# Held loads, spaced GpSimd work, later step sizes, and two expert tiles returned by TensorE

## The chip, the cores and the metric

The kernel runs on one core of one Trainium2 chip. Its engines are TensorE (PE in the profile, PEld for its weight loads), VectorE (DVE), ScalarE (ACT), GpSimd (POOL) and SyncE (SP, which here only issues DMAs). The metric is device time in microseconds of one execution. Times are compared as medians of several runs.

## The reference

The input x has 1024 tokens of 512 features, all in fp32. Six residual blocks follow, each on a layer-normalized x; the expert layer appears twice with the same weights.

```python
x = x + 0.5 * _L0_ffn_ref(_layernorm(x), W_gate, b_gate, W_e, b_e)      # f0
x = x + _L0_attn_ref(_layernorm(x), wq, wkv, wo)                        # 32 heads, causal
x = x + 0.5 * _L0_ffn_ref(_layernorm(x), W_gate, b_gate, W_e, b_e)      # f1
x = x + 0.5 * _L1_ffn_ref(_layernorm(x), W_up, gate_w, ..., lora_B)     # up projection + LoRA expert
x = x + _L1_attn_ref(_layernorm(x), in_proj_w, ..., out_proj_w)         # Mamba, 64 heads, 8 groups
x = x + 0.5 * _L1_ffn_ref(_layernorm(x), W_up, gate_w, ..., lora_B)

def _L0_ffn_ref(x, W_gate, b_gate, W_e, b_e):          # 8 experts, two per token
    logits = x @ W_gate + b_gate
    _, top_idx = jax.lax.top_k(logits, 2)
    y_all = jax.nn.relu(jnp.einsum('bsd,edh->bseh', x, W_e) + b_e)
    y = jnp.take_along_axis(y_all, top_idx[..., None], axis=2)
    return y.mean(axis=2)
```

In the Mamba block the step size of each token and head is `dt_p = softplus(dt + dt_bias)` and its decay `exp(dt_p * A)`, with `dt` a projection to 64 columns; a scan over the tokens uses both.

## The kernel before

x stays in chip memory as eight tiles of 128 tokens (`x`), and `hT` holds the transposed, normalized x (four blocks of 128 features by 1024 tokens). `wpool` has four buffers of 1 MB for weights, `psml` four PSUM banks and `pbig` two double ones. Instructions are written in one text, but their order on an engine is worked out when the program is built: an instruction may go ahead of one that stands earlier in the text, unless `queue_behind` (one behind another) or `keep_in_program_order` pins it.

**An expert layer** (`expert_ffn`, tag f0 or f1) computes only the chosen experts. The normalized rows are stored to the DRAM tensor `rows`. DVE computes for every token its two experts and a place in a list of rows sorted by expert and padded to tiles of 128, the slot tiles. There are at least 16 slot tiles (`NS0`) and at most 23 (`NS`); a chain of `tc.If` skips those that are not used. `token` (L537) says for each slot which row to take, and `gather` (L543) fetches a tile's rows by an indirect DMA on POOL's queue; an unused place gets row 0. `turn` (L558) transposes a tile on PE and `slot_tile` (L593) multiplies it by its expert's weights, chosen by a register: eight PE instructions of 512 columns, a bias addition on DVE (L610), ReLU on ACT (L616) and a store to the DRAM tensor `outs` (L617). Tiles run in the order of their numbers. A tile's expert lies within bounds, so tile s up to 7 needs experts 0 to s loaded, and later ones all eight.

In f0, `gates_of_input` issues all loads on SP's queue: experts 0 to 3, then the row stores with experts 4, 5 after the fourth and 6, 7 after the eighth, then the biases, 2 MB spread over the partitions. The attention's first weights (`load_first`) are held back by `hold` (L160): a small memset into the tile on POOL, pinned to its place in POOL's queue, which the load must wait for. `meanwhile` is a list of pieces of other work: `load_first`, then two scalings of w_q (L806) and four sums or differences (L781) on POOL. The loop over the tiles takes one after tile 1 and one after each even tile from 4. After tile 2, SP also writes finite values into the rows of `outs` that belong to tiles 16 to 22, from x (L627).

**The way back.** `collect` (L667) makes a pipeline over the eight token tiles, used by the attention's first value projection after f0 and by the LoRA layer after f1: per tile two indirect gathers from `outs` (`gather_row`, L652), two additions into x on DVE (`add_pair`, L683), normalization (`normalize`, with the root as a power on POOL, L173), a transpose into `hT`, and then the next layer's products.

**The Mamba block** (`mamba`) goes over 16 units, a group of eight heads by half the sequence, four chunks of 128 tokens each. A unit begins with five `project_pair` calls (16 PE instructions of 512 columns each), of which three end in a convolution and SiLU (`conv_silu`: ACT, then DVE L1310), and `finish_bc`. Each chunk has `prepare` (the decays read back from DRAM into `dd`, a scan on DVE for `e_seg`, L1414) and `scan` (products, y). Ahead of the units, the pipeline after f1 ends in `add_bias` (L1253), which collects the step sizes; after token tile 3 and after tile 7 it calls `steps_of_time(q)` (L1185) for its half of the sequence: softplus and decays on DVE and ACT, three cumulative sums (`ps_cum`) and eight transposes on PE, and two stores to DRAM (`decay`) on SP's queue. Only after that does the text load group 0 and begin unit 0 (`load_group(0)` and five `project_pair`, at the end of `mamba`). The pools `w2` (xdt, xw, y and others) and `ep` (dd, e, cs) are opened after the pools of the step sizes are closed, on the memory these leave.

Of the kernel before, what the change touches and what calls it, by code (L numbers as in the profile page):

```python
# [22 lines left out]
P = 128  # L23
S = 1024
D = 512
# [11 lines left out]
NS0 = 2 * S // P  # L37
NE1 = 4
# [38 lines left out]
def macaron_kernel(  # L77
# [32 lines left out]
    rows = dram.tile([S, D], F32, tag="rows", name="rows")  # L110
# [49 lines left out]
    def hold(w):  # L160

        tc.keep_in_program_order(nc.gpsimd.memset(w[0:1, :, 0:1], 0.0))

    def weights(src, name, held=False):
        w = wpool.tile([P, KT, D], F32, tag="w", name=name)
        if held:
            hold(w)
        nc.sync.dma_start(w, src.rearrange("(k p) c -> p k c", p=P))
        return w
# [156 lines left out]
    def store_rows(t, xn):  # L326
        nc.scalar.dma_start(rows[t * P : (t + 1) * P, :], xn)

    def gate_steps(keep=store_rows, own=None):
# [6 lines left out]
        )  # L336

    def expert_ffn(tag, meanwhile, behind_weights=lambda: None):
# [5 lines left out]
        with tc.tile_pool(name=f"{tag}wa", bufs=1) as wap, tc.tile_pool(  # L344
# [16 lines left out]
            def gates_of_input():  # L361


                def keep(t, xn):
                    tc.keep_in_program_order(
                        nc.sync.dma_start(rows[t * P : (t + 1) * P, :], xn)
                    )
                    if t % 4 == 3:
                        for e in range(4 + t // 2 - 1, 4 + t // 2 + 1):
# [14 lines left out]
            behind_weights()  # L384

# [17 lines left out]
            nc.gpsimd.iota(lane_i, pattern=[[0, 1]], base=0, channel_multiplier=1)  # L403
# [137 lines left out]
            gathered, turned = {}, {}  # L541

            def gather(s):  # L543
                if s < NS0 + 3:
# [3 lines left out]
                nc.gpsimd.indirect_dma_start(  # L548
# [4 lines left out]
                    bounds_check=S - 1,  # L553
# [4 lines left out]
            def turn(s):  # L558
                xs = gathered.pop(s)
                ps = transposes(lambda i: xs[:, i * P : (i + 1) * P], KT)  # L560
                if s < NS0:
# [6 lines left out]
            for s in range(2):  # L568
                gather(s)

# [21 lines left out]

            def slot_tile(s):  # L593
                if s + 1 < NS:
                    turn(s + 1)
# [5 lines left out]
                for k in range(KT):  # L601
# [6 lines left out]
                    )  # L608
                y = wk.tile([P, D], F32, tag="y", name="y_e")
                nc.vector.tensor_tensor(  # L610
                    y,
                    ps,
                    b_all[:, bass.ds(ev, 1), :].rearrange("p e c -> p (e c)"),
                    ALU.add,
                )
# [1009 lines left out]
```

## Time and profile before

| | |
|---|---|
| median of 3 runs | 2866.86 us (2865.0 to 2867.82) |
| the profiled execution | 2867.5 us; its span 2865.8 us |
| PE busy | 2757.0 us (96%), mean granted clock 0.983 |
| DVE, ACT, POOL busy | 1747.1, 700.7, 901.6 us |
| DMA, mean over the span | 69 GB/s |
| slot tiles that ran (stores `outs<-y_e`) | 40: 19 in f0 and 21 in f1 |

A line of the timeline or of the groups reads: start in us and duration, engine, line of the kernel, operation, written tile <- read tiles, sizes, how many instructions; in brackets the idle time of that engine just before it and what ended it. PEq, SPq and the like are an engine's sequencer. A fp32 product of 128x128 by 128x512 is two instructions. POOL's DMA_INDIRECT is the issue of a gather, not its landing. The granted clock is 1.0 when PE runs at full speed.

### The profile page before, as it was taken

The page shows a single profiled execution, that of the slowest core. Times are in us where ns is not written, and L with a number is a line of the kernel's source. Part 1 is how long each engine was busy: PE and PEld are TensorE (multiplying, and loading weights), DVE is VectorE, ACT ScalarE, POOL GpSimd, SP SyncE. Part 2 cuts the span into 40 slices and gives each one's busy share as a digit, 9 for nine tenths or more (in the row PEclk, how much of TensorE's full clock was granted, in tenths as well). Part 3 has the DMA queues.
Part 4 walks back from the last instruction along what each step waited for, and adds up shares of the span by engine and source line. Part 5 has one row for each costly group of instructions (what it writes and reads, how often), then busy time and mean ns, then how long its engine had stood idle before and what let it go on. Part 6 is the DMA issues. An engine that isn't in the chain of part 4 may idle for free. (4 is left out here: it accounts for less than half of the span.)

```text
span 2865.8 us, 30223 instructions
## 1 busy us (share of the span) xinstructions
PE 2757.0 (96%) x11027; PEld 1567.6 (55%) x11027; DVE 1747.1 (61%) x3203; ACT 700.7 (24%) x1368; POOL 901.6 (31%) x749
## 2 busy tenths in 40 slices
PE   5799999999999999999999779999999999999998
PEld 3345566665666656666555434455555555555554
DVE  3256555665555656556555236767777776767673
ACT  2222221222222222212222224322223232222320
POOL 4322112221121212212200330355554545555451
PEclk8899999999999999999999889999999999999999
DMA  9411001010100101001014431223232222223210
GB/s 349 128 41 30 15 22 38 16 30 15 32 28 15 30 15 44 15 15 30 15 37 176 129 114 55 91 76 117 91 100 81 102 97 89 96 88 117 96 45 30
DMA packets 99604, 197.28 MB, mean 69 GB/s; under 512 B 8112, under 2 KB 33888, under 8 KB 99200
## 3 DMA queue, kind: packets, MB, share of 16 engines
q1 hardware_dynamic: 84944, 161.08, 17.1%
q0 software_dynamic: 6304, 20.47, 2.7%
q10 hardware_dynamic: 8208, 13.78, 1.3%
q8 instruction: 90, 1.47, 0.2%
q14 instruction: 58, 0.48, 0.1%
HBM read 176.17 MB, written 19.14 MB: 68 GB/s over the span
## 5 line engine op out<-in xcount | busy, mean ns | idle before, releaser
L855 PE MATMUL ps_s<-kT,qT 128*128 128x512 f32 (+3 forms) x768 | 292.8, 488 | 0.1
L879 PE MATMUL ps_o<-pT,v 128*128 128x512 f32 (+3 forms) x768 | 258.6, 486 | 0.2 <-ACT pT L900 0.2
L900 ACT COPY pT<-ps_tr 128x256 f32<-128x256 f32 (+2 forms) x192 | 91.7, 478 | 646.9 <-PE ps_tr L181 635.1
L869 ACT ACTIVATE pr<-ps_s,nm 128x128 f32<-128x128 f32 (+7 forms) x256 | 190.4, 744 | 238.4 <-DVE nm L866 208.0
L1509 PE MATMUL ps_out<-w_out,yg 128*128 128x512 f32 x512 | 237.2, 606 | 1.0 <-DVE yg L1472 1.0
L1439 POOL TENSOR_TENSOR cs<-cT,dd 128x1024 f32<-128x1024 f32 x56 | 181.9, 3248 | 167.9 <-PE ps_y L1457 139.6
L267 PE MATMUL ps_in<-hT,w_g 128*128 128x512 f32 x512 | 225.8, 594 | 1.5 <-ACT dt_ln L1196 1.5
L267 PE MATMUL ps_in<-hT,w_x 128*128 128x512 f32 x512 | 225.4, 592 | 0.0
L879 PEld LDWEIGHTS ps_o<-pT,v 128*128 128x128 f32 x768 | 143.5, 190 | 144.8 <-issue 98.8
L866 DVE TENSOR_REDUCE nm<-ps_s 128x1 f32<-128x128 f32 (+7 forms) x256 | 192.5, 753 | 3.9
L181 PEld LDWEIGHTS ps_tr<-ident,pr 128*128 128x128 f32 x1152 | 136.2, 141 | 76.3 <-issue 44.9
L181 PE MATMUL ps_tr<-ident,pr 128*128 128x128 f32 x1152 | 170.6, 275 | 4.3 <-DVE pr L871 3.2
L871 DVE TENSOR_SCALAR pr<-pr,sm 128x128 f32<-128x128 f32 (+7 forms) x256 | 165.6, 647 | 7.4
L267 PEld LDWEIGHTS ps_in<-hT,w_x 128*128 128x128 f32 x512 | 97.1, 190 | 121.2 <-issue 121.0
L267 PEld LDWEIGHTS ps_in<-hT,w_g 128*128 128x128 f32 x512 | 96.5, 190 | 121.6 <-issue 119.3
L1414 DVE TENSOR_TENSOR_SCAN e_seg<-dd,eye 128x1024 f32<-128x1024 f32 x64 | 154.5, 2414 | 6.4 <-PE ps_y L1457 6.3
L1310 DVE SCALAR_TENSOR_TENSOR xc<-ps_in,conv,xc 128x511 f32<-128x511 f32 (+2 forms) x192 | 141.7, 738 | 18.3 <-ACT xc L1306 17.9
L855 PEld LDWEIGHTS ps_s<-kT,qT 128*128 128x128 f32 x768 | 127.5, 192 | 39.9 <-issue 26.8
L1509 PEld LDWEIGHTS ps_out<-w_out,yg 128*128 128x128 f32 x512 | 93.0, 192 | 94.8 <-issue 94.3
L953 POOL TENSOR_TENSOR so<-oT 128x256 f32<-128x256 f32 x28 | 20.0, 725 | 380.2 <-DVE oT L886 336.7
L1433 POOL TENSOR_TENSOR xw<-xdt,erev 128x512 f32<-128x512 f32 x56 | 59.3, 1059 | 244.9 <-DVE xdt L1427 215.1
L806 POOL TENSOR_SCALAR w_q<-w_q 128x1024 f32<-128x1024 f32 x16 | 44.3, 2771 | 291.5 <-DMA w_q<-in_wq_dram 291.1
(290 smaller groups left out, 4823.7 us busy)
## 6 DMA issues: line engine op xcount, KB each, us to landing
dd<-decay SPq DMA_DIRECT2D x128, 512.0 KB, 4.6
w_all<-in_w_e_dram SPq DMA_DIRECT2D x16, 1024.0 KB, 12.4
outs<-y_e ACTq DMA_DIRECT2D x40, 256.0 KB, 3.6
w_v<-in_wkv_dram SPq DMA_DIRECT2D x8, 1024.0 KB, 5.2
w_q<-in_wq_dram SPq DMA_DIRECT2D x32, 256.0 KB, 4.2
w_k<-in_wkv_dram SPq DMA_DIRECT2D x8, 1024.0 KB, 5.2
w_o<-in_wo_dram SPq DMA_DIRECT2D x8, 1024.0 KB, 5.2
w_x<-in_in_wt_dram SPq DMA_DIRECT2D x8, 1024.0 KB, 7.8
```

Source lines behind the costliest of these rows:

```text
L181: nc.tensor.transpose(ps[:, i * P : (i + 1) * P], src(i), ident)
L267: nc.tensor.matmul(ps[:, cols : cols + n], lhsT=w[:, k, c0 : c0 + P], rhs=hT[:, k, t0 : t0 + n], start=(k == 0), stop=(k == KT - 1),)
L855: nc.tensor.matmul(ps[:, j : j + m], lhsT=qT[:, qt * P : (qt + 1) * P], rhs=kT[:, j : j + m], start=True, stop=True,)
L866: nc.vector.tensor_reduce(nm, ps[:, :n], AX.X, ALU.max, negate=True)
L869: nc.scalar.activation(pr[:, :n], ps[:, :n], AF.Exp, bias=nm, accum_out=sm)
L871: nc.vector.tensor_scalar(pr[:, :n], pr[:, :n], sm, None, ALU.mult)
L879: nc.tensor.matmul(ps[:, lo:512], lhsT=v[:, kb, hh * P : (hh + 1) * P], rhs=pT[:, kb, lo:512], start=(kb == 0), stop=(kb == last),)
L900: nc.scalar.copy(dst, src)
L1310: nc.vector.scalar_tensor_tensor(dst[:, s:], ps[:, : half - s], conv[:, ct, 3 - s : 4 - s], dst[:, s:], ALU.mult, ALU.add,)
L1414: nc.vector.tensor_tensor_scan(e.rearrange("p h l -> p (h l)"), dd[:, 0, :], eye8.rearrange("p h l -> p (h l)"), 0.0, ALU.mult, ALU.add,)
L1439: nc.gpsimd.tensor_tensor(cs, un["cT"][:, tok].unsqueeze(1).to_broadcast([P, HPG, P]), dd[:, 1, :].rearrange("p (h l) -> p h l", l=P), ALU ...
L1509: nc.tensor.matmul(po, lhsT=yg[:, k, :], rhs=w_o[:, k, :], start=(k == 0), stop=(k == 3))
```

## The change

- **Loads.** In f0 experts 6 and 7 and the biases leave the place among the row stores. They are issued after the first two gathers in the text, each behind a memset on POOL (`hold`, which now gets the slice to write).
- **GpSimd work.** In f0 the pieces of `meanwhile` behind `load_first` are taken one per tile from the eighth tile on, each pinned behind the gather that this step of the loop issues.
- **Two last tiles.** Slot tiles 6 and 7 (`LAST`), which are always in use, run after all others. Their gathered rows have buffers of their own, zeroed on POOL in f0; in f0 SP stores these zeros to their rows of `outs`, so that the two gathers of the way back fetch zeros for them. Their output is not stored: it stays in `hT` (`returned`). DVE builds matrices with a one where slot row and token belong together (`whose`, also in `hT`), and `return_last` adds the product of both to each token tile. `rows` gets a row 0 of its own and tokens count from 1, so that an unused place belongs to no token.
- **Step sizes.** `steps_of_time(1)` is called after the five `project_pair` and `finish_bc` of unit 0, which move ahead with `load_group`, `conv_silu` and the other helpers (their text is unchanged but for `in_line["conv"]`). The first scan of group 0 is pinned behind the last convolution.

```diff
+LAST = (6, 7)
-    rows = dram.tile([S, D], F32, tag="rows", name="rows")
+    rows = dram.tile([1 + S, D], F32, tag="rows", name="rows")
     def hold(w):
-        tc.keep_in_program_order(nc.gpsimd.memset(w[0:1, :, 0:1], 0.0))
+        tc.keep_in_program_order(nc.gpsimd.memset(w, 0.0))
...
+    def returned(s):
+        k = 2 * LAST.index(s)
+        return hT[:, k : k + 2, 6 * P :]
+
+    def whose(t):
+        k, c = (0, t) if t < 6 else (2, (5, 4)[t - 6])
+        return hT[:, k : k + 2, c * P : (c + 1) * P]
...
-                    if t % 4 == 3:
-                        for e in range(4 + t // 2 - 1, 4 + t // 2 + 1):
+                    if t == 3:
+                        for e in range(4, 6):
                             tc.keep_in_program_order(load_expert(e))
...
+                tc.keep_in_program_order(nc.sync.dma_start(rows[0:1, :], x[0:1, 0, :]))
                 Tiles(*gate_steps(keep, own)).flush()
-                tc.keep_in_program_order(load_biases())
...
+            last_rows = {
+                s: rp.tile([P, D], F32, tag=f"own{s}", name="xs_own") for s in LAST
+            }
+            if tag == "f0":
+                for s in LAST:
+                    nc.gpsimd.memset(last_rows[s], 0.0)
+            order = [*(s for s in range(NS0) if s not in LAST), *range(NS0, NS)]
+            follows = dict(zip(order, order[1:]))
...
             for s in range(2):
                 gather(s)
+            if tag == "f0":
+
+                hold(b_all[0:1, :, 0:1])
+                hold(w_all[0:1, 6:, 0, 0:1])
+                tc.keep_in_program_order(load_biases())
+                for e in range(6, NE):
+                    tc.keep_in_program_order(load_expert(e))
...
+            numbers = rp.tile([P, len(LAST)], F32, tag="numbers", name="numbers")
+            nc.vector.tensor_scalar(
+                numbers, token[:, LAST[0] : LAST[-1] + 1], -1.0, None, ALU.add
+            )
+            within = rp.tile([P, len(LAST), NT], F32, tag="within", name="within")
+            nc.vector.tensor_tensor(
+                within,
...
+            for t in range(NT):
+                nc.vector.tensor_tensor(
+                    whose(t),
+                    lanes.unsqueeze(1).to_broadcast(pairs_of),
+                    within[:, :, t : t + 1].to_broadcast(pairs_of),
+                    ALU.is_equal,
+                )
...
+                if s in LAST:
+                    y = returned(s)
+                    two = "p (k c) -> p k c"
+                    nc.vector.tensor_tensor(
+                        y, ps.rearrange(two, k=2), b.rearrange(two, k=2), ALU.add
+                    )
+                    nc.scalar.activation(y, y, AF.Relu, scale=0.25)
+                    return
...
-            for s in range(NS0):
-                for i in range(s + 2, NS if s == NS0 - 2 else min(s + 3, NS)):
-                    if i not in gathered and i > 1:
-                        gather(i)
+            static = [s for s in range(NS0) if s not in LAST]
+            for i, s in enumerate(static):
+                if s == static[-2]:
+                    ahead = [*range(NS0, NS), *LAST]
+                else:
+                    ahead = static[i + 2 : i + 3]
+                for j in ahead:
+                    gather(j)
                 slot_tile(s)
+                if s == static[-2]:
+                    for j in LAST:
+                        turn(j)
...
+                    for j in LAST:
+                        tc.keep_in_program_order(
+                            nc.sync.dma_start(outs[j * P : (j + 1) * P, :], last_rows[j])
+                        )
-                if (s == 1 or s > 3 and s % 2 == 0) and meanwhile:
+                if tag == "f0":
+
+                    if s == 1:
+                        meanwhile.pop(0)()
+                    elif i > 6 and meanwhile:
+                        queue_behind(meanwhile.pop(0)(), issued[ahead[0]])
+                elif (s == 1 or s > 3 and s % 2 == 0) and meanwhile:
                     meanwhile.pop(0)()
...
                     more_tiles.enter_context(tc.If(n > s))
                     slot_tile(s)
+            for s in LAST:
+                slot_tile(s)
...
+    def return_last(t):
+
+        ps = psml.tile([P, 512], F32, tag="ps", name="ps_ret")
+        w = whose(t)
+        for i, s in enumerate(LAST):
+            nc.tensor.matmul(
+                ps, lhsT=w[:, i, :], rhs=returned(s), start=(i == 0), stop=(s == LAST[-1])
+            )
+        nc.vector.tensor_tensor(x[:, t, :], x[:, t, :], ps, ALU.add)
...
             pairs[t] = make()
             gather_row(t, 0)
+            return_last(t)
...
-                    if t % nh == nh - 1:
-                        steps_of_time(t // nh)
+                    if t == nh - 1:
+                        steps_of_time(0)
...
+                gr = load_group(0)
+                un = begin_unit(gr, 0)
+                for j in range(5):
+                    project_pair(un, j)
+                    if j == 1:
+                        finish_bc(un)
+                steps_of_time(1)
...
-                nc.vector.tensor_tensor_scan(
+                segments = nc.vector.tensor_tensor_scan(
                     e.rearrange("p h l -> p (h l)"),
...
+                if c == 0 and un["g"] == 0:
+                    queue_behind(segments, in_line["conv"])
```

More of the change, by code (lines that the diff above doesn't have):

```diff
@@ L326, in store_rows @@
     def store_rows(t, xn):
-        nc.scalar.dma_start(rows[t * P : (t + 1) * P, :], xn)
+        nc.scalar.dma_start(rows[1 + t * P : 1 + (t + 1) * P, :], xn)
     def gate_steps(keep=store_rows, own=None):
@@ L365, in keep @@
                     tc.keep_in_program_order(
[L366 removed]
+                        nc.sync.dma_start(rows[1 + t * P : 1 + (t + 1) * P, :], xn)
                     )
[L368 to L369 removed]
+                    if t == 3:
+                        for e in range(4, 6):
                             tc.keep_in_program_order(load_expert(e))
@@ L560, in turn @@
                 ps = transposes(lambda i: xs[:, i * P : (i + 1) * P], KT)
-                if s < NS0:
+                if s < NS0 and s not in LAST:
                     xt = wk.tile([P, KT, P], F32, tag="xt", name="xt_s")
@@ L591, in expert_ffn @@
             nc.vector.tensor_copy(n_i, ends[:, NE - 1 :])
+            numbers = rp.tile([P, len(LAST)], F32, tag="numbers", name="numbers")
[5 more added lines that the diff above has]
+                within,
+                numbers.unsqueeze(2).to_broadcast([P, len(LAST), NT]),
+                steps[:, :NT].unsqueeze(1).to_broadcast([P, len(LAST), NT]),
+                ALU.subtract,
+            )
+            pairs_of = [P, len(LAST), P]
+            for t in range(NT):
[5 more added lines that the diff above has]
+                )
             def slot_tile(s):
-                if s + 1 < NS:
-                    turn(s + 1)
+                if s in follows:
+                    turn(follows[s])
                 xt = turned.pop(s)
@@ L1518, in mamba @@
             units = [(g, hf) for g in range(MG) for hf in range(2)]
-            gr = load_group(0)
-            un = begin_unit(gr, 0)
-            for j in range(5):
-                project_pair(un, j)
-                if j == 1:
-                    finish_bc(un)
             ready = prepare(un, 0)
```

207 lines of the change are left out of this document (103 added, 104 removed).

## The prediction

> **What bounds the kernel now.** The page first: PE is busy 96% of a span of 2865.8 us, and its busy slices read 9 nearly everywhere. So a change pays only where PE stands still or runs at a lowered clock. The table of stages finds these places (columns: window, its length, then busy time and count of PE, PEld, DVE, ACT, POOL; granted clock; DMA share; GB/s):
>
> ```profile
> 20.00:40.00 20.00, 3.20 (x35) 2.01 (x31) 10.93 (x40) 0.56 (x3) 4.25 (x4) 0.64 1.05 406
> 120.00:140.00 20.00, 4.70 (x16) 2.54 (x15) 8.11 (x16) 2.05 (x4) 10.20 (x11) 0.70 0.40 118
> 1670.00:1700.00 30.00, 16.22 (x49) 7.70 (x48) 8.71 (x15) 5.49 (x9) 8.68 (x12) 0.80 0.27 88
> 1795.00:1800.00 5.00, 1.44 (x4) 0.37 (x2) 5.00 (x6) 0.00 (x0) 1.36 (x1) 1.00 0.57 210
> 1800.00:1805.00 5.00, 2.88 (x7) 2.21 (x8) 4.19 (x9) 3.65 (x6) 0.00 (x0) 0.53 0.01 3
> ```
>
> They are the entry of the first expert FFN (f0), the ends of both FFNs, and the entry of the Mamba stage. Only these are touched, so I read each in the timeline. The entry of f0, and the same step of the second FFN (f1):
>
> ```profile
> 34.65 1.19 POOL L548 DMA_INDIRECT xs<-rows,token  x1 [18.47 <-DVE of_f L583]
> 43.29 2.34 PE L181 MATMUL ps_tr<-ident,xs 128*128 128x128 f32 x8 [9.93 <-DMA xs<-rows,token]
> 50.99 0.69 DVE L610 TENSOR_TENSOR y_e<-ps_e,b_all 128x512 f32<-128x512 f32 x1 [16.11 <-PE ps_e L602]
> ...
> 1595.93 1.15 POOL L548 DMA_INDIRECT xs<-rows,token  x1 [16.66 <-DVE past L574]
> 1599.50 1.09 PE L181 MATMUL ps_tr<-ident,xs 128*128 128x128 f32 x4 [4.30 <-DMA xs<-rows,token]
> ```
>
> From the start of the first row gather to the first transpose it is 8.64 us in f0 and 3.57 us in f1. In f0 the DMA engines are full (share 1.05) with expert weights and biases.
>
> The ends of f0 and f1:
>
> ```profile
> 122.77 0.69 DVE L610 TENSOR_TENSOR y_e<-ps_e,b_all 128x512 f32<-128x512 f32 x1 [3.18 <-PEq L637]
> 127.24 1.01 POOL L654 DMA_INDIRECT pair<-outs,slot_i  x1 [22.21 <-issue]
> 135.74 1.09 PE L181 MATMUL ps_tr<-ident,ln_xn 128*128 128x128 f32 x4 [13.07 <-DVE ln_xn L199]
> 139.97 6.04 PE L278 MATMUL ps_v<-w_v,hT 128*128 128x512 f32 x8
> 146.29 3.60 PE L278 MATMUL ps_v<-w_v,hT 128*128 128x512 f32 x8
> ...
> 1698.92 1.09 PE L181 MATMUL ps_tr<-ident,ln_xn 128*128 128x128 f32 x4 [13.78 <-DVE ln_xn L199]
> ```
>
> PE waits for bias, ReLU, store, gather and normalization, then starts at half clock: eight ps_v take 6.04 us and later 3.60. Entry of Mamba:
>
> ```profile
> 1789.33 7.11 PE L267 MATMUL ps_in<-hT,w_g 128*128 128x512 f32 x16 [1.45 <-ACT dt_ln L1196]
> 1789.40 4.44 DVE L1414 TENSOR_TENSOR_SCAN e_seg<-dd,eye 128x1024 f32<-128x1024 f32 x1
> 1802.12 1.19 PE L1222 MATMUL ps_cum<-dta,upper 128*128 128x256 f32 x2 [5.69 <-DVE dta L1213]
> 1808.18 7.03 PE L267 MATMUL ps_in<-hT,w_g 128*128 128x512 f32 x16
> ```
>
> The second half's step sizes stand on PE's queue ahead of the last projection, and their DVE chain is late, behind two scans.
>
> **Part 1, held loads (entry of f0).** Removed from the time before the first gather: experts 6 and 7 (1 MB each) and the biases (2 MB), 4 MB in all; they now follow memsets that stand behind the first two gathers on POOL's queue. At the 406 GB/s of the table 4 MB are 10 us of DMA time, more than the 8.64 - 3.57 = 5.07 us by which the gather is late, so I take f1's 3.57: gain 5.07. Against it: two memsets of 128x512 on POOL in the set-up. 128x128 takes 0.20 to 0.24 us, so one is between 0.24 and 0.96, two 0.5 to 1.9, ahead of the first root (L173 at 6.97, input ready at 6.20); DVE has other statistics to do meanwhile. I take 0.7 (0 to 2.0). The biases leave at about 37.5; 2 MB at 406 GB/s plus a gather's 3.57 end near 46.2, when the first bias addition is due (50.99 - 4.4 = 46.6). If later, a tile of 3.87 us is covered by the four PSUM banks; without it each us counts. The experts are first needed seven tiles on. Ten small DVE operations for the selection matrices (128x256: between 0.29 of L482's 128x128 and 0.62 of L521's 128x512; 0.42 taken, about 4 us) lie in DVE's idle 16.11: nothing. The store of row 0 is 2 KB ahead of SP's row stores: nothing. Net -4.4 (-5.1 to -1.5).
>
> [...]
>
> **Part 2, spaced POOL work.** At 65.45 to 74.96 four differences (L781) run in one go; the gather behind them starts at 75.10 and PE waits 1.28 + 0.30 us near 79. One after each gather removes that: -1.5 (-1.6 to 0). New: the gathers of tiles 6 and 7 also wait for the zero stores that read their tiles, and these are last on SP's queue, behind 1.8 MB for `outs` that landed at 75.5. Whatever is behind them on POOL waits too, the next rows above all. They are needed some 12 tiles in, beyond 90 us: +1 (0 to +8).
>
> **Part 3, the last two tiles (ends of f0 and f1).** Added on PE: a 128x128x512 product is two instructions (eight for four k, 3.60 us with the last one's tail, 0.43 from start to start); a return has two products, 1.72 us; eight make 13.75 per FFN, 27.5 in all. What they may fill, f0: idle 13.07 + 2.23 (ahead of the second transpose at 139.06), and half clock: 2.44 for ps_v, 1.0 for two transposes: 18.7. f1: 13.78 + 0.68, and 2.5 for two transposes, one gate and one ps_up group at half clock: 17.0. The gather chain now starts while PE computes tiles 6 and 7 (eight instructions, 3.44 us, each). New idle: the branch's join, after which in f1 POOL was released at 1686.09, 1.0 behind the last matmul, so 1.1; and bias 0.69 plus ReLU 0.63 of tile 7 with hand-over, 1.5. So 13.75 + 2.6 = 16.4 each: -2.3 and -0.6, together -2.9. The first transpose: return 1.72, its addition 0.69, two pair additions, statistics, root and scaling some 5 us: all behind four returns, so PE stays busy. Engines do not keep the text's order (the cast of L591 runs at 27.60, ahead of L482 at 27.71), so the ends: nothing idle, -8.2; or, where PE's queue holds a transpose ahead of the later returns and DVE does the returns' additions ahead of the pairs, 3.3 more idle and 3 at half clock in each, +9.7. DVE's new 8 x 0.69 per FFN fit: it had 3.4 us a tile, now 4.1, under PE's 5.6. The zero-store and the shifted row numbers cost no instruction here.
>
> [...]
>
> **Part 4, step sizes behind the first unit.** PE's idle 1.45 + 5.69, and half clock from 1802.12 to 1808 (the same products took 0.67, 0.59, 0.59 in the first half and now 1.19, 1.06, 1.06; with the transposes and the B-C products 3.1): 10.2 at stake. [...] Moved with it: three ps_cum, two groups of transposes, two stores on SP ahead of the next decay loads (needed four chunks on). The pool of y opens on memory that the step sizes use, so y still waits for them. I take -7 (-10.2 to 0).
>
> **Sum.** -4.4 - 1.5 + 1 - 2.9 - 7 = -14.8. The profiled execution took 2867.5 (span 2865.8 and 1.7 around), the median is 2866.86: 2852.
>
> **Rivals.** *Memory of the step sizes keeps the Mamba entry as it is* (part 4 does not do what it says): the scan of chunk 0 cannot store y, DVE at 100% in 1795 to 1800 speaks for it, the free PE work against: 2852 + 7 = 2859. *The returns eat all they hide*, part 3 at its worse end: 2852 + 12.6 = 2865; for it, the join and the serial chain. *Slower: the returns come on top.* If the first transposes are no earlier and PE takes the 27.5 us outside the gaps, the other parts' -11.9 are outweighed: 2866.9 - 11.9 + 27.5 = 2882. It decides from 17.6 us uncovered, two thirds of the products (5.7 us are the 0.2% that a measurement tells from nothing). Against it: the idle is there, and the inputs of a return come from chip memory, not through a store.
>
> **Chances.** Forecast 0.56 (2844 to 2861), Mamba entry unchanged 0.19, returns eat their room 0.13, on top 0.12. Of the second two thirds are over 0.2% faster, so faster 0.68, same 0.20, slower 0.12. Leaving out the last and little more, the range is 2843 to 2867.
>
> **What would show it.** First transpose of f0 at 38 to 40; no PE gap near 79; 32 product pairs with ones-matrices, idle before them under 3 us and clock 1.0 in the windows of both ends; no ps_cum wait between the projections of unit 0. Wrong if the first gather still takes 8 us, if PE waits for rows in mid-f0, or if idle before the first transpose of a tail stays over 8 us with the returns behind it.

## The result: 5.5 us slower

| | median, us | runs |
|---|---|---|
| before | 2866.68 (2862.67 to 2871.42) | 18 |
| changed | 2872.19 (2867.18 to 2877.28) | 18 |
| ratio | 1.0018, 95% interval 1.0011 to 1.0025 | |

The forecast was 2852. The profiled execution of the changed kernel took 2875.0 us, with a span of 2873.2. Its windows at the places that the prediction read, from the table of stages (window, its length, busy time and count of PE, PEld, DVE, ACT, POOL; granted clock; DMA share; GB/s):

```profile
80.00:100.00 20.00, 14.98 (x38) 7.01 (x38) 2.13 (x4) 3.54 (x7) 13.13 (x9) 0.83 0.54 186
128.00:148.00 20.00, 15.30 (x42) 6.72 (x41) 12.88 (x25) 1.98 (x4) 12.87 (x13) 1.00 0.43 118
1682.00:1712.00 30.00, 25.18 (x61) 10.89 (x60) 12.63 (x23) 4.91 (x8) 11.34 (x14) 0.94 0.30 89
1805.00:1810.00 5.00, 3.88 (x10) 1.58 (x9) 4.93 (x11) 4.21 (x5) 0.00 (x0) 1.00 0.00 0
1810.00:1815.00 5.00, 5.00 (x12) 2.14 (x12) 5.00 (x8) 2.76 (x4) 0.00 (x0) 1.00 0.15 40
```

Both FFN ends and the entry of Mamba look as forecast: PE is busier and its clock is at or near 1.0. But busy here includes the 27.5 us of new return products. And a stage that nobody had on the list, 80 to 100, now has 5 us of idle and a clock of 0.83. Before the change the same stretch was nearly full:

```profile
80.00:100.00 20.00, 19.73 (x61) 9.85 (x62) 3.24 (x5) 5.66 (x11) 5.05 (x5) 1.00 0.53 144
```

To see where time was won and lost, I compared the same points in both timelines, one profiled execution each (us from the start of the span; I call them anchors):

| anchor | before | changed | shift |
|---|---|---|---|
| first transpose of slot rows, f0 | 43.29 | 39.18 | -4.1 |
| last slot tile of f0 ends | 122.67 | 130.2 | +7.5 |
| first product of attention (ps_m) | 172.52 | 179.90 | +7.4 |
| last output projection of attention, first addition (on DVE) | 1546.26 | 1555.43 | +9.2 |
| last slot tile of f1 ends | 1685.14 | 1696.8 | +11.7 |
| first ps_in of Mamba | 1755.98 | 1768.59 | +12.6 |
| end of the span | 2865.8 | 2873.2 | +7.4 |

The entry gives 4.1 us and Mamba about 5; the slot tiles of f0 take 11.6 between the first two rows of the table, and the rest is spread. Nearly all of the 11.6 lies at two places: at 92 us 5.02 us of idle and 2.2 of slow products behind it, and ahead of the last two tiles 2.08 of idle, where the branches join, and 1.8 of slow products. The entry and the loss on PE, in the timeline of the changed kernel:

```profile
39.18 1.09 PE L183 MATMUL ps_tr<-ident,xs 128*128 128x128 f32 x4 [4.85 <-DMA xs<-rows,token]
...
83.72 3.67 PE L654 MATMUL ps_e<-w_all,xt_s 128*128 x8
92.42 1.08 PE L183 MATMUL ps_tr<-ident,xs 128*128 128x128 f32 x4 [5.02 <-DMA xs<-rows,token]
93.33 5.75 PE L654 MATMUL ps_e<-w_all,xt_s 128*128 x8
...
121.39 8.82 PE L654 MATMUL ps_e<-w_all,xs_own 128*128 x16 [2.08 <-ACTq L711]
```

and POOL's queue in the same stage:

```profile
85.70 1.03 POOL L572 DMA_INDIRECT xs_own<-rows,token  x1 [6.28 <-DMA outs<-xs_own]
87.04 1.02 POOL L572 DMA_INDIRECT xs_own<-rows,token  x1 [0.30 <-issue]
88.36 1.01 POOL L572 DMA_INDIRECT xs<-rows,token  x1 [0.30 <-issue]
89.41 2.35 POOL L868 TENSOR_TENSOR sqk<-sqk,w_q 128x1024 f32<-128x1024 f32 x1
```

Read it from PE back: at 92.42 PE had been idle for 5.02 us, waiting for the rows of an ordinary slot tile. Their gather was issued at 88.36, behind the two gathers of tiles 6 and 7 (`xs_own`). The first of these had waited 6.28 us for the zero stores that read the same tile (`outs<-xs_own`). After the idle the next eight products take 5.75 us instead of 3.60; the granted clock is 0.50 from 92.3 to 97.3 us, half clock for the larger part of them, and 0.98 from 97.3 to 102. The text puts the gathers of tiles 6 and 7 at the end of the static tiles; in the queue that runs they stand at 85 us, ahead of rows that PE needs first.

### The profile page after: what moved, and what is told of

Its sections match the earlier page's. It is cut to its first block, busy times and chain, and to the rows that moved or that the text cites. A ratio compares the mean times of both kernels' runs of the same rounds, so it can differ in the third digit from the quotient of the medians.

```text
span 2873.2 us, 30372 instructions
## 1 busy us (share of the span) xinstructions
PE 2787.8 (97%) x11091; PEld 1579.4 (55%) x11091; DVE 1757.0 (61%) x3239; ACT 705.2 (25%) x1371; POOL 903.0 (31%) x753
## 5 line engine op out<-in xcount | busy, mean ns | idle before, releaser
L183 PEld LDWEIGHTS ps_tr<-ident,pr 128*128 128x128 f32 x1152 | 136.9, 142 | 75.7 <-issue 44.9
```

The source lines that it names most:

```text
L183: nc.tensor.transpose(ps[:, i * P : (i + 1) * P], src(i), ident)
```

## The experiments

"Before" is measured anew beside each group of runs: 2866.58 us for e1 to e4, 2866.70 for e5 to e8, 2866.08 for e9 and e10, 2867.59 for e11 and e12. A difference is of medians, against the "before" of its group; the 95% intervals of the ratios in brackets are 2 to 4 us wide to each side, so differences of 1 or 2 us between experiments mean little. In the changed kernel it was +5.5.

### e1_no_returns: the changed kernel without its last two tiles

```diff
-LAST = (6, 7)
+LAST = ()
...
-            return_last(t)
```

> The changed kernel without its last two tiles: LAST is empty, the zero stores, the eight one-hot products' operands and the return products are gone, all slot tiles go the old way; held loads, spaced GpSimd work and the step sizes behind the first unit stay. Theory: these three parts gain what the anchors of TensorE showed, 4.1 + 1.6 + 5.2 = 10.9 us, so about 2856 us beside 2866.7, and all of the loss lies in the part that is left out. Rival: part of the loss lies in the other parts (the held weights arrive too late for attention, or the moved step sizes cost what they save elsewhere): 2862 us or more.

2856.03 us (2854.96 to 2856.11), ratio 0.9962 [0.9948, 0.9976]: -10.6, where -10.9 was expected; the same kernel once more (e12) gave -9.3. So the sum holds: the whole loss, 16.2 us (14.8 by e12), lies in the last two tiles and what belongs to them. That the three parts share the 10.6 as the anchors suggested is not shown by this run (e8, e10 and e11 deny it).

### e2_own_zeros: the zeros in a tile that nobody fills, or so I thought

```diff
-                for s in LAST:
-                    nc.gpsimd.memset(last_rows[s], 0.0)
+                zeros = more_rows.tile([P, D], F32, tag="own", name="zeros")
+                nc.gpsimd.memset(zeros, 0.0)
...
-                            nc.sync.dma_start(outs[j * P : (j + 1) * P, :], last_rows[j])
+                            nc.sync.dma_start(outs[j * P : (j + 1) * P, :], zeros)
```

> The changed kernel, but the zeros that are stored into outs come from a tile of their own, so that the gathers of tiles 6 and 7 need not wait until the two stores have read the tiles that they fill. Theory: the 6.28 us that GpSimd waited at 85.70 us is gone, the gathers behind it are issued in time, the 5.02 us idle of TensorE at 92.42 us and its half clock go with it, and the time falls by about 8 us against the changed kernel, to about 2864 us. Rival: the rows are late because the queue on SP is full of weights and the stores, whatever they read: the gathers' landing stays late, TensorE still idles some 5 us near 92 us, time about 2871 us.

2870.45 us, ratio 1.0015 [1.0006, 1.0024]: +3.9, near the rival's number. But POOL's timeline says why:

```profile
86.62 1.03 POOL L572 DMA_INDIRECT xs_m<-rows,token  x1 [7.62 <-DMA outs<-zeros]
87.95 1.01 POOL L572 DMA_INDIRECT xs<-rows,token  x1 [0.30 <-issue]
```

I had taken the zeros from a pool of four rotating buffers, and one of the late slot tiles (`xs_m`) comes round to the same buffer. The gathers of tiles 6 and 7 now run at 46.10 and 47.41 without a wait; the wait only changed its victim. So the run does not decide between theory and rival; it does show that in both kernels the gather that fills what the stores read stops POOL (6.28 us in the changed kernel, 7.62 here), and PE again idles 4.89 us at 91.90.

### e5_zeros_apart: the zeros in memory that no gather fills

```diff
-                for s in LAST:
-                    nc.gpsimd.memset(last_rows[s], 0.0)
...
+                zeros = rp.tile([P, n2, P], BF16, tag="at_row", name="zeros")
+                nc.gpsimd.memset(zeros[:, : n2 // 2, :], 0.0)
+                zeros = zeros[:, : n2 // 2, :].rearrange("p i c -> p (i c)").bitcast(F32)
...
-                            nc.sync.dma_start(outs[j * P : (j + 1) * P, :], last_rows[j])
+                            nc.sync.dma_start(outs[j * P : (j + 1) * P, :], zeros)
```

> The changed kernel with the zeros in memory that no gather fills (that of at_row, which is read for the last time before the first gather), written once behind the holds; in e2_own_zeros the zeros shared a rotating buffer with a later slot tile, and GpSimd still waited 7.62 us for outs<-zeros, so that run could not decide. Theory: now no gather waits for the two stores, the wait near 86 us is under 0.5 us, TensorE's 5 us of idle time at 92 us go, the last slot tile ends near 122 us instead of 130, and the time is about 2864 us. Rival: the gathers land late because the queues are full with the held weights and the stores: TensorE still idles 4 us or more near 92 us and the time stays near 2871 us.

2862.73 us (2860.41 to 2868.33), ratio 0.9988 [0.9979, 0.9997]: -4.0, and 9.5 less than the changed kernel. POOL, and then the table of stages for 80 to 100:

```profile
46.77 1.02 POOL L569 DMA_INDIRECT xs_own<-rows,token  x1 [0.30 <-issue]
...
82.32 1.03 POOL L569 DMA_INDIRECT xs<-rows,token  x1 [0.16 <-issue]
83.37 2.38 POOL L867 TENSOR_TENSOR sqk<-w_q,sqk 128x1024 f32<-128x1024 f32 x1
86.11 1.03 POOL L569 DMA_INDIRECT xs<-rows,token  x1 [0.36 <-PE ps_tr L183]
```

```profile
80.00:100.00 20.00, 20.00 (x69) 10.35 (x68) 3.46 (x5) 6.64 (x12) 11.03 (x7) 1.00 0.65 217
```

The stores are the same, behind the same weights on SP's queue, issued at 68.02 us (69.36 in the changed kernel), and land 12.5 and 17.7 us after their issue; from 68 to 86 us the DMA engines are as full as before (share 1.04, 0.98 in the changed kernel). What is gone is the dependency, and with it the place of the two gathers: they run at 46.77 and 48.09 now, no longer at 85.70 and 87.04. PE is busy for all 20 us at a granted clock of 1.00 and the last slot tile ends at 122.6. The rival (full queues) falls. The expected 2864 was within 1.3 us. The dependency, with the place that it gave the two gathers, was worth 9.5 us by the medians (8.6 by the ratios; 7.6 in the two traces at the end of the last tile).

The early place has a price of its own: a row that PE wants at 52.54 is now late by 2.72 us. And the execution that was profiled took 2867.99, 5.3 us above this kernel's median, so its later anchors are read with care.

### e3_pairs_first: where the pairs of the way back lie in memory

```diff
-        with tc.tile_pool(name=f"{tag}wa", bufs=1) as wap, tc.tile_pool(
...
+        with tc.tile_pool(name=f"{tag}w", bufs=3) as wk, tc.tile_pool(
...
-        with tc.tile_pool(name="a_v", bufs=2) as vp, tc.tile_pool(
...
+        with tc.tile_pool(name="a_p", bufs=3) as pp, tc.tile_pool(
```

> The changed kernel with another order of memory: the pool of the slot tiles' working buffers is opened ahead of the expert weights, and in attention the pool that holds the pairs is opened first, so that the pairs lie over working buffers and no longer over expert weights and biases which the last tile still reads. Nothing else differs, and the stage ahead of Mamba keeps its order of reading. Theory: the first gather of the way back waited for the bias addition of tile 7 only because its pair lies on that memory; it now starts at about 125 us instead of 131.2, as soon as the last stores have landed, and the time falls by 4 to 6 us against the changed kernel, to about 2867 us. Rival: the wait comes from the join of the branches, not from memory: the gather still starts at 131 us behind the same bias addition, and the time stays at 2872 us.

2875.2 us, ratio 1.0030 [1.0019, 1.0040]. The first gather of the way back and the first transpose behind it, in the changed kernel:

```profile
131.22 1.01 POOL L740 DMA_INDIRECT pair<-outs,slot_i  x1 [29.80 <-DVE hT L665]
...
140.14 0.66 PE L183 MATMUL ps_tr<-ident,ln_xn 128*128 128x128 f32 x4 [3.06 <-DVE ln_xn L201]
```

and here:

```profile
124.99 1.01 POOL L742 DMA_INDIRECT pair<-outs,slot_i  x1 [22.72 <-issue]
...
136.73 0.94 POOL L175 TENSOR_TENSOR ln_rs<-ln_rs,neg_half 128x1 f32<-128x1 f32 x1 [5.46 <-DVE ln_rs L174]
...
138.37 0.66 PE L183 MATMUL ps_tr<-ident,ln_xn 128*128 128x128 f32 x4 [1.84 <-DVE ln_xn L201]
```

The mechanism is shown: with the pairs on other memory the gather no longer waits for the bias addition of tile 7 (`DVE hT L665`) and starts 6.2 us earlier, while PE is still on tiles 6 and 7. Its expected worth is not: the first transpose comes only 1.8 us earlier (1.2 against the end of the last tile), because DVE now makes the roots wait. The gain in time failed to appear. In the trace f1, whose pools were reordered too, lost what f0 won: its first transpose waited 8.47 us for rows instead of 4.63, and from there to the end of its last tile it took 90.1 us instead of 86.6. That the order of the pools is the cause there was not tried apart.

### e6_both: e5_zeros_apart, and the pairs of attention alone moved

```diff
...
+            if tag == "f0":
+                wk = pool("w", 3)
             wap, rp, more_rows = pool("wa", 1), pool("r", 1), pool("m", 4)
+            if tag == "f1":
+                wk = pool("w", 3)
...
-        with tc.tile_pool(name="a_v", bufs=2) as vp, tc.tile_pool(
+        with tc.tile_pool(name="a_p", bufs=3) as pp, tc.tile_pool(
...
```

> The kernel of e5_zeros_apart, and in the first expert stage the working buffers ahead of the weights, with the pairs of attention on their memory (e3_pairs_first without its change of the second expert stage, which there lost some 3 us). Theory: in e3_pairs_first the gather chain started 6.2 us earlier, but the first transposed rows came only 1.2 us earlier against the end of the last tile, since the return products and VectorE's additions of them now stand ahead: so 1 to 2 us less than e5_zeros_apart, about 2862.5 us. Rival: the order of memory costs or gains nothing at all: equal to e5_zeros_apart.

2862.5 us, ratio 0.9988 [0.9979, 0.9996]: equal to e5_zeros_apart (2862.73) by the medians. In the traces the first gather starts at 116.5 instead of 123.6 and the stretch from the end of the last tile to attention's first product is 48.5 instead of 49.7 us; 1.2 us is less than the medians of such scattered runs can show.

### e7_no_product: what the return products cost

The body of `return_last` is left out: the rows of tiles 6 and 7 do not come back into x, so the later stages work on other values (the slot tiles of f1 took 85.9 us, 86.6 in the changed kernel).

```diff
     def return_last(t):
-        ps = psml.tile([P, 512], F32, tag="ps", name="ps_ret")
...
-        nc.vector.tensor_tensor(x[:, t, :], x[:, t, :], ps, ALU.add)
+        return
```

> The changed kernel with the return products and their additions to x left out: the rows of slot tiles 6 and 7 don't come back, the rest is as in the changed kernel. It measures what the 27.5 us of return products cost. Theory: in the first tail they replaced idle time and half clock but for some 3.5 us (last tile's end to first product of attention 49.85 us with them; without them 1.1 us to the gather chain, 8.5 us to the first transposition and 36.8 us from there, as before the change, 46.4 us), in the second about as much: time about 2865 us. Rival 1: they are hidden wholly: 2872 us. Rival 2: they lie on the path: 2845 us.

2862.37 us, ratio 0.9985 [0.9976, 0.9993]: 9.8 less than the changed kernel. From the end of the last tile to the next stage's first product: f0 44.9 us instead of 49.7, f1 67.8 instead of 71.8. So of 27.5 us of products some 18 replaced idle time and half clock and the rest, together with DVE's additions, is paid, more than the 7 expected and far from either rival.

### e9_last_ahead: the two tiles ahead of the branches

```diff
+            for s in LAST:
+                slot_tile(s)
             with ExitStack() as more_tiles:
...
-            for s in LAST:
-                slot_tile(s)
```

> The kernel of e5_zeros_apart with slot tiles 6 and 7 ahead of the branched tiles instead of behind them. Theory: the idle time of TensorE at the join of the branches (2.08 us in the first expert stage, 0.79 in the second) no longer stands ahead of two tiles of work, but the gather chain of the way back again waits until the branched tiles' stores have landed, 4.6 us behind the last tile instead of 1.0, so that the first transposition comes 13.1 us behind it instead of 10.0: the two cancel, time within 2 us of 2862.7. Rival: the place behind the branches is what the return products cost, and 4 us or more are gained: 2858 us.

2866.74 us, ratio 0.9996 [0.9987, 1.0005]: no gain on e5_zeros_apart (-4.0 there, +0.7 here by the medians, 2.3 us apart by the ratios, with intervals that overlap), so the rival falls; whether the theory's "within 2 us" holds, these runs can't tell. The join is paid in either place:

```profile
121.90 7.13 PE L732 MATMUL ps_ret<-hT 128*128 128x512 f32 x16 [2.08 <-ACTq L712]
133.82 1.12 PE L183 MATMUL ps_tr<-ident,ln_xn 128*128 128x128 f32 x4 [4.79 <-DVE ln_xn L201]
134.73 3.62 PE L732 MATMUL ps_ret<-hT 128*128 128x512 f32 x4
```

The same 2.08 us now stand ahead of the returns, and behind the gap of 4.79 four return instructions take 3.62 us, where those of the changed kernel at 140.63 take 1.88 at a granted clock of 1.00. So it isn't their place behind the branches that costs.

### e4_steps_only: the step sizes alone

The kernel before with the Mamba stage of the changed one:

```diff
-                    if t % nh == nh - 1:
-                        steps_of_time(t // nh)
+                    if t == nh - 1:
+                        steps_of_time(0)
...
+                gr = load_group(0)
+                un = begin_unit(gr, 0)
+                for j in range(5):
+                    project_pair(un, j)
+                    if j == 1:
+                        finish_bc(un)
+                steps_of_time(1)
...
```

> The kernel before with one part of the change alone: the step sizes of the second half stand behind the first unit's projections. Theory by the anchors: 5.2 us less than before, 2861.5 us; the prediction's term was 7, 2860 us. Rival: TensorE loses the same idle time elsewhere in Mamba: no difference from 2866.7 us.

2860.58 us (2858.49 to 2863.16), ratio 0.9977 [0.9968, 0.9987]: -6.0, between the anchors' 5.2 and the predicted 7. PE in the window that had idled 5.69 us:

```profile
1797.10 7.13 PE L267 MATMUL ps_in<-hT,w_g 128*128 128x512 f32 x16 [1.11 <-ACT sg L1249]
1804.07 0.59 PE L1345 MATMUL ps_cum<-dta,upper 128*128 128x256 f32 x2
```

There is no wait ahead of ps_cum, and it takes 0.59 us; before it took 1.19, at a granted clock of 0.50 (1802 to 1805 us).

### e8_held_only and e10_spaced_only: the held loads and the spacing, each alone

```diff
# e8_held_only, kernel before
...
-                    if t % 4 == 3:
-                        for e in range(4 + t // 2 - 1, 4 + t // 2 + 1):
+                    if t == 3:
+                        for e in range(4, 6):
...
-                tc.keep_in_program_order(load_biases())
...
+            if tag == "f0":
+                hold(b_all[0:1, :, 0:1])
+                hold(w_all[0:1, 6:, 0, 0:1])
+                tc.keep_in_program_order(load_biases())
+                for e in range(6, NE):
+                    tc.keep_in_program_order(load_expert(e))
```

```diff
# e10_spaced_only, kernel before
...
-                if (s == 1 or s > 3 and s % 2 == 0) and meanwhile:
+                if tag == "f0":
+                    if s == 1:
+                        meanwhile.pop(0)()
+                    elif s > 6 and meanwhile:
+                        queue_behind(meanwhile.pop(0)(), issued[s + 2])
...
```

> The kernel before with the held loads alone: biases and experts 6 and 7 wait for two marks that GpSimd writes behind the first two gathers. Theory by the anchors: 4.1 us less, plus up to 1 us since the memsets of the own tiles are not there: 2862 us, first transposition of slot rows near 38.6 us instead of 43.3. [...]

2873.41 us (2871.76 to 2874.78), ratio 1.0021 [1.0012, 1.0030]: +6.7: slower, where the theory had 2862. The first transpose is at 38.44, as expected. What follows it, on SP (and the same four issues before the change), on POOL and on PE:

```profile
43.05 20.00 SPq L799 DMA_DIRECT2D w_q<-in_wq_dram  x4
```

```profile
46.25 3.70 SPq L794 DMA_DIRECT2D w_q<-in_wq_dram  x4
```

```profile
68.30 5.63 POOL L811 TENSOR_SCALAR w_q<-w_q 128x1024 f32<-128x1024 f32 x2 [7.79 <-DMA w_q<-in_wq_dram]
74.20 1.09 POOL L547 DMA_INDIRECT xs<-rows,token  x1 [0.27 <-issue]
...
84.87 1.04 POOL L547 DMA_INDIRECT xs<-rows,token  x1 [0.16 <-issue]
```

```profile
80.93 1.09 PE L181 MATMUL ps_tr<-ident,xs 128*128 128x128 f32 x4 [6.66 <-DMA xs<-rows,token]
81.86 6.02 PE L607 MATMUL ps_e<-w_all,xt_s 128*128 x8
```

The 4 MB that were held back now stand on SP's queue just ahead of attention's weights: the four issues of w_q take 20.00 us of SP's time, where before the change they took 3.70 (46.25 to 49.95). POOL reaches the scaling of w_q and waits 7.79 us for it. The row gather at 74.20, for PE's next tile, stands behind that wait and the two scalings, and its rows take 6.73 us more to reach PE (the DMA engines are full, share 1.03 from 60 to 81 us): PE idles 6.66 us ahead of 80.93 and then needs 6.02 us for eight products that take 3.60 in the tile before. The next gather, at 84.87, stands behind four differences in one go and costs PE 0.50 + 0.29 us. The 4.9 us won at the entry are gone and 5.2 more by the end of the last slot tile (127.82, before 122.67).

> The kernel before with the spaced GpSimd work alone (one piece behind each gather from slot tile 7 on). Theory: without the held loads the weights of attention arrive early enough, and what spacing gains is the 1.28 + 0.30 us that TensorE waited near 79 us: 2865 us. Since e8_held_only lost 6.7 us and held loads with spacing, with the step sizes moved, gained 10.6 us, of which the step sizes are 6.1, spacing is worth some 11 us with the held loads and less than 2 without. Rival: spacing gains several us by itself: 2860 us or less.

2862.6 us (2859.68 to 2867.23), ratio 0.9987 [0.9978, 0.9996]: -3.5, between theory (-1.6) and rival (-6); the interval, -6.3 to -1.1, excludes neither. The spaced pieces leave no gap of PE between 60 us and the last tile, which ends 2.7 us earlier. Of these 2.0 lie at the old gap near 79 us, and 0.7 at the entry, which the edit does not touch: there the transposes and first products took 6.39 us instead of the 7.67 of before, where the granted clock was 0.50 from 43.3 to 48 us.

### e11_spaced_steps and e12_no_returns_again: are the held loads worth anything?

e11 is the kernel before with the edits of e10 and of e4; e12 is e1 once more, which has the held loads besides (and the store of row 0 and the shifted row numbers of the change).

> The kernel before with the spaced GpSimd work and the moved step sizes, without the held loads and without the last two tiles. Theory: spacing alone gained 3.5 us and the step sizes alone 6.1, so 9.6 us less, 2856.9 us, and the held loads, which brought the first slot tile forward by 4.7 us, keep at most 1 us of it, because rows of later slot tiles then arrive late. Rival: the held loads keep their 4 us, and this kernel needs 2860 us or more.

> The kernel of e1_no_returns once more, on the chip of e11_spaced_steps, so that the two differ by the held loads alone. Theory: 2856 us, at most 1 us below e11_spaced_steps. Rival: 3 to 4 us below it.

On one chip, without the held loads 2857.87 us (2854.77 to 2860.42; ratio 0.9968 [0.9955, 0.9980]), with them 2858.30 (2855.59 to 2859.96; 0.9963 [0.9949, 0.9977]). The held loads bring nothing that can be measured here, and the 3 to 4 us of the rival fall; with five and six runs that scatter by 4 to 6 us, a gain of 2 us would not show. At the end of f0's last tile the two stand at 119.65 and 119.23, though the first transposes were at 43.49 and 38.24. Of the 5.25 us of lead 2.6 are gone when the first tile's products end (49.95 and 47.31): the second tile's rows came late (PE idles 1.18 us for them), and the first tile's eight products took 5.90 us in e12, 4.69 in e11. Another 2.2 go near 79 us, where POOL had waited for w_q and the row gather behind the scaling was late:

```profile
68.87 2.78 POOL L869 TENSOR_SCALAR w_q<-w_q 128x1024 f32<-128x1024 f32 x1 [4.35 <-DMA w_q<-in_wq_dram]
```

```profile
79.76 0.63 PE L183 MATMUL ps_tr<-ident,xs 128*128 128x128 f32 x4 [1.47 <-DMA xs<-rows,token]
```

Both beat the kernel before by 9 to 10 us, and so the changed kernel by some 15. Spaced GpSimd work with the moved step sizes is the version to keep, and the simpler one.

## Why the prediction was wrong

The terms, as predicted for the end of the span and as run (medians):

| term | predicted | measured | from |
|---|---|---|---|
| part 1, held loads | -4.4 | +6.7 alone, about 0 beside part 2 | e8, e11 and e12 |
| part 2, spacing | -1.5 | -3.5 alone (-6.3 to -1.1) | e10 |
| part 2, gathers wait for the zero stores | +1 | +9.5 (8.6 by the ratios) | changed kernel less e5 |
| part 3, last two tiles, without that wait | -2.9 | +6.7 (+5.3 by e12) | e5 less e1 |
| part 4, step sizes | -7 | -6.0 | e4 |

With parts 1 and 2 together at -4.6 (e1 less e4) the rows add up to -4.6 + 9.5 + 6.7 - 6.0 = +5.6. They must: the four differences form a chain from before to changed, so that this sum tests nothing. It shows where the 20 us between -14.8 and +5.5 lie. Two terms failed, and by about as much: the wait for the zero stores (+1 predicted, +9.5) and the last two tiles (-2.9 predicted, +6.7).

**Part 2, the first failed step.** "New: the gathers of tiles 6 and 7 also wait for the zero stores that read their tiles ... Whatever is behind them on POOL waits too, the next rows above all": the mechanism was named, but given +1 with an end of +8, because the rows were "needed some 12 tiles in, beyond 90 us". Two things were missed. The stores are not done near 75, where `outs<-x` landed before; behind the held weights SP issues them only at 69.36, and POOL is released at 85.70. And what is queued behind them is needed at once: the gather issued at 88.36 was that of PE's very next tile, the twelfth, which was due at 87.40. PE idled 5.02 us, and the slow products behind it (5.75 us for 3.60) came on top. "Engines do not keep the text's order" stood in the prediction, for another step; here the two gathers ran ahead of rows that the text puts first.

**Part 1** was right where it looked and wrong in its sum. From the first gather to the first transpose it fell from 8.64 to 3.56 us, a gain of 5.08 where 5.07 was forecast. The two memsets cost 0.97 (0.7 forecast): the first gather started at 35.62 instead of 34.65. That the loads made the first rows late is shown by e8: with this edit alone the first transpose came at 38.44 instead of 43.29. What failed is "The experts are first needed seven tiles on", as if the 4 MB were the only thing that comes later. Attention's weights stand behind them on SP, POOL's scaling waits for these, and the row gathers wait for POOL. The held loads delayed what stood behind them on their queue (four issues of w_q in 20.00 us in e8, 3.70 before), not themselves alone.

**Part 2's spacing**, -1.5, counted the one wait that the trace of before shows, and that is 2.0 us in e10's trace; the medians say -3.5, with an interval that holds both. Beside the held loads it is worth some 11 (from +6.7 to -4.6), since rows then pass between the late pieces. So parts 1 and 2 without the zero stores came near their forecast (-4.6 for -5.9) by luck: each alone was something else, and the gain is that of the spacing (e11).

**Part 3, the second failed step,** had the wrong sign. "The gather chain now starts while PE computes tiles 6 and 7" did not happen in f0: it started at 131.22, released by tile 7's bias addition, since its buffer lies on memory which that addition's stage still uses (e3). That cost little (1.2 us in e6's trace). The larger miss is what the 27.5 us of products would fill: 18.7 + 17.0 with 2.6 of new idle each. In f0 the idle behind the last tile was to shrink to 1.5; 3.06 + 1.64 remained, and the stretch from the end of the last tile to attention's first product is 49.8 us before and 49.7 after, no gain. In f1 the stretch to the first ps_in is 70.8 us before and 71.8 after. With the idle ahead of the last two tiles (2.08 in f0 and 0.79 in f1, 1.1 forecast for each) that is +1.9 and +1.8 where -2.3 and -0.6 were forecast. The chain of one tile on DVE grew. Three additions, statistics and scaling are 4.01 us from root to root, 3.54 and then 3.4 before; and the returns' additions of the next two tiles (0.68 each) run ahead of the first tile's statistics. The roots before and changed, and PE's wait for the second tile:

```profile
134.01 0.94 POOL L173 TENSOR_TENSOR ln_rs<-ln_rs,neg_half 128x1 f32<-128x1 f32 x1 [0.34 <-DVE ln_rs L172]
137.55 0.81 POOL L173 TENSOR_TENSOR ln_rs<-ln_rs,neg_half 128x1 f32<-128x1 f32 x1
```

```profile
138.50 0.94 POOL L175 TENSOR_TENSOR ln_rs<-ln_rs,neg_half 128x1 f32<-128x1 f32 x1 [0.80 <-DVE ln_rs L174]
142.51 0.95 POOL L175 TENSOR_TENSOR ln_rs<-ln_rs,neg_half 128x1 f32<-128x1 f32 x1 [0.34 <-DVE ln_rs L174]
```

```profile
144.15 0.66 PE L183 MATMUL ps_tr<-ident,ln_xn 128*128 128x128 f32 x4 [1.64 <-DVE ln_xn L201]
```

e7 puts the bill at 9.8 us for products and additions. In the changed kernel's trace half clock also followed the join in f0 (granted 0.50 from 121.4 to 124.4 us; 8.82 us for 16 instructions, 7.13 in e5). The rival "The returns eat all they hide", with part 3 at +9.7 and the join and the serial chain named for it, is the nearest to what came; e5 less e1 says +6.7. How the +6.7 divide was read from single traces and not tried apart. In those of e5 and e1, 12.0 us apart in their spans, the tiles of f0 take 4.4 us more (the join, and the late row at 52 us), the gates of f1 1.9 (eight gate products in 1.12 us, 0.66 in e1), its tiles 2.5, the two ends 0.4 and 1.5. "On top" (27.5) did not happen.

**Part 4** was right: the wait of 5.69 us is gone, ps_cum takes 0.59 us at a granted clock of 1.00 (1790 to 1820 us in the changed kernel), and the size, -6.0 for -7, agrees within the noise (interval -9.2 to -3.7). The 3 us that -7 leaves of the 10.2 at stake were an estimate of mine that no run shows; what the traces of e4 and of the changed kernel show is a new wait of 1.11 us for ScalarE ahead of the last projection (`ACT sg`). The rival of unchanged Mamba falls.

The prediction's own list of what would prove it wrong had "if PE waits for rows in mid-f0". It did.

## What to carry to other kernels

When a load is held or a dependency is added, follow the queue and not the item: list what stands behind it on its DMA queue and on its engine until the first thing that the bound engine needs, and price that. Give constants that are stored early memory that nothing later fills; one shared buffer cost 9.5 us here, and a rotating pool only moved the wait. A sum of differences that form a chain always closes; only an edit that is run alone, as e8 and e10 were, shows what it is worth. Work that fills an idle gap is free only if the chain that made the gap does not grow with it: here each filled tile added an addition of 0.68 us to the very chain that PE was waiting for (4.01 us from root to root, 3.54 before).

## What was unexpected about the hardware

After the same short idle the same code ran at two clocks. In the last head of attention, code that the change does not touch, PE idles 1.75 and 1.40 to 1.41 us in every profile. These are the eight transposes behind the second idle, in e1_no_returns and in its repetition e12, the same kernel:

```profile
1531.74 1.54 PE L183 MATMUL ps_tr<-ident,pr 128*128 128x128 f32 x8 [1.41 <-DVE pr L934]
```

```profile
1532.67 1.06 PE L183 MATMUL ps_tr<-ident,pr 128*128 128x128 f32 x8 [1.41 <-DVE pr L934]
```

They took 1.06 or 1.07 us in seven of fourteen profiles and 1.43 to 1.94 in the other seven (in the changed kernel 1.94, at a granted clock of 0.50 from 1542.3 to 1544.1 us; before 1.06, at 1.00 from 1535.6 to 1536.8), and the slow ones need 1375.35 to 1376.31 us from attention's first product to its last projection, the fast ones 1372.96 to 1374.13. The profile before was a fast one and that of the changed kernel a slow one: that is the +1.8 between these two points in the table of anchors. Since e1 and e12 show both, it can belong to the execution alone. Whether an edit makes it likelier stays open: the four profiles without the held loads (before, e4, e10, e11) are all among the fast seven. A term of 2 us read from one profile should therefore be checked at a second one before it is blamed on an edit.

The other surprise is the 20.00 us that SP needed to issue w_q's four loads behind 4 MB more of weights (3.70 before the change; 20.05 in the changed kernel, 18.43 in e5). All that stood behind them on SP went out later: the store `outs<-x` at 67.35 us instead of 56.91. What SP waited for, the traces do not name.
